# Attention and feed-forward on one core: additions at a batch's end in later steps, and products that nobody reads at the kernel's end

## The chip, the cores and the metric

The kernel runs on one core of a Trainium2 chip. The metric is the device time of one execution in microseconds (us); lower is better. Engine names follow the profile: PE is TensorE's matrix products, PEld its weight loads, DVE is VectorE, ACT is ScalarE, POOL is GpSimd, SP is SyncE, which issues most DMAs.

## The reference

`x` is 8 batches of 1024 rows of 128 numbers, all in float32. Each row is normalised, and attention with 8 query heads and one shared key and value head, and a linear feed-forward sum over 8 experts, are both added to the row:

```python
xn = _layernorm(x, axis=-1)
Q = jnp.einsum('bnd,hdk->bhnk', xn, proj_q)      # 8 heads
K = jnp.einsum('bmd,dk->bmk', xn, proj_k)
V = jnp.einsum('bmd,dv->bmv', xn, proj_v)
weights = softmax(jnp.einsum('bhnk,bmk->bhnm', Q, K), axis=-1)
O = jnp.einsum('bhnm,bmv->bhnv', weights, V)
attn = jnp.einsum('bhnv,hdv->bnd', O, proj_o)
mid = jnp.einsum('amh,ehn->aemn', xn, w1)        # no activation in between
ffn = jnp.einsum('aemn,enh->amh', mid, w2)
out = x + attn + ffn
```

Shapes: `proj_q`, `proj_o` (8, 128, 128), `proj_k`, `proj_v` (128, 128), `w1` (8, 128, 512), `w2` (8, 512, 128).

## The kernel before

Weights are multiplied together once at the start: queries and keys into one matrix per head (`wqk`), values and output into one per head (`wvo`), all experts into one 128x128 matrix (`wf`). After that the work is a single loop over 512 steps: 8 batches x 8 heads (a head of a batch is a unit `u`) x 8 blocks of 128 rows. The order of the instructions on every engine is the order in which the code writes them; nothing is rearranged by a scheduler, and semaphores are set by the framework.

Step `i` does, in this order:

- `logits(i)`: TensorE multiplies one block of 128 query rows with 1024 keys (`logits_half` twice, recorded at helper line L103) into a score tile `pl` in PSUM; VectorE takes the row maximum (`row_max`, L354); ScalarE computes the exponents and their sum (`exponents`, L360, with a second small instruction that reads the accumulated sum).
- `weights_t(i - 1)`: VectorE turns the divided rows of the step before in 32x32 blocks (L377). Every fourth step SP then moves the blocks with 16 DMAs (L405) into the tiles `g0` and `g1`.
- `divide(i)`: VectorE takes the reciprocal of the sums (L370), ScalarE multiplies the rows by it (L371).
- `run(...)`: TensorE takes the next one or two pairs of products from a list of jobs, 12 steps behind (`LAG`). The product of weights and values is cut into seven block products in place of eight, so POOL forms sums and differences of `g0` and `g1` (`sum_early` L423, `sums_late` L428, L429, L431), and the products (L453) of all heads of a batch gather in four PSUM accumulators, `acc0` to `acc3`. `PAIRS = (2, 2, 1, 2)` says how many pairs a step takes.
- every eighth step `queries` for the unit after next (copied out by ScalarE at L305), and four steps later `values` (copied out at L323 and L324).
- `collect(b, n)`: additions that bring the accumulators of a finished batch together.

Scores, queries and values share the PSUM pool `ps_sc`, which has two slots, used in turn (`slot`). `queries` and `values` stand behind the logits of their step, so the logits of the next step get the slot of the logits just before.

A column half is 64 of the 128 columns of the stationary matrix: `both_halves` writes the lower and the upper 64 output partitions with two products. `lo` and `hi` are these partitions in `collect` as well.

The end of batch `b` is counted by `b, r = divmod(i - 69, 64)`. Step `r` runs the parts that `COLLECT` lists, last in the step:

```python
COLLECT = {0: [0], 2: [1], 3: [2, 3], 4: [4], 6: [5], 7: [6, 7, 8], 8: [9], 10: [10], 11: [11]}
```

Parts 0 and 2 are copies on ScalarE; all others are additions on VectorE of one PSUM and one SBUF operand, 64 partitions by 512. Part 5 adds the lower half of `acc1` (L531), 6 its upper half (L533), 7 its lower half into upper partitions (L535); 8 and 9 (L538, L540) read the lower half of `acc2`, 10 (L542) its upper and 11 (L544) its lower half again. Part 7 reads what 6 wrote, 8 what 5 wrote, 9 what 7 wrote, 10 what 6 wrote, 11 what 10 wrote. At r = 15 the sums are turned and moved, and later added to `x` and stored. The table applies to batches 0 to 6. For batch 0, r = 6 is step 75; `values` stands in step 76 (r = 7), `queries` in step 80 (r = 11).

The last batch ends in `last_rows`: eight transposes (L622) and four products with `spread` (L631) into four PSUM tiles, additions to `x` (L638), and two DMAs out for each half, issued by SP and ACT (L643). They are the last work of the kernel; then the closing of the framework (L881) waits for all engines and landings.

Of the kernel before, what the change touches and what calls it, by code (L numbers as in the profile page):

```python
# [9 lines left out]
F32 = mybir.dt.float32  # L10
# [7 lines left out]
def kernel(  # L18
# [42 lines left out]
    nc = tc.nc  # L61
    ctx.enter_context(tc.manual_schedule())
    P = 128
    HP = P // 2
# [5 lines left out]
    NE, _, NF = w1.shape  # L70
    NB = S // P
    GN = 4
    GS = GN * P
# [16 lines left out]
    ps_acc = ctx.enter_context(tc.tile_pool(name="ps_acc", bufs=1, space=PSUM))  # L90
# [22 lines left out]
    xs, xns, xnTs, qTs, vfs = {}, {}, {}, {}, {}  # L113

    def chunked(t):

        return t.rearrange("(c p) d -> p c d", p=P)

    def rows_tile(name):
        return rows.tile([P, NB, D], F32, tag="rows", name=name)  # L120
# [50 lines left out]
    for e in range(2):  # L171
# [6 lines left out]
    ident = const.tile([P, P], F32, tag="ident", name="ident")  # L178
# [6 lines left out]
            name=nc.get_next_instruction_name(), act_func_set_id=EXP_AND_LN, ins=[], outs=[]  # L185
# [239 lines left out]
    def sums_late(u, engine):  # L425
        x1, x2 = key_half(g0s[u], 0), key_half(g0s[u], 1)
        y1, y2 = key_half(g1s[u], 0), key_half(g1s[u], 1)
        engine.tensor_sub(x1, y1, x1)  # L428
        engine.tensor_sub(x2, f1s[u], y1)  # L429
        f4s[u] = form("f4", u)  # L430
        engine.tensor_sub(f4s[u], y2, x2)  # L431
# [62 lines left out]
    def in_order(t):  # L494
        return t.rearrange("p (r t q) -> p t r q", r=NQ, q=Q)

    def by_query(t):
        return t.rearrange("p (t r q) -> p t r q", t=GN, q=Q)

    def collect(b, n):  # L500

        if n == 0:
            tiles = [rows_tile(f"end{k}_{b}").rearrange("p a b -> p (a b)") for k in range(2)]
            ends[b] = [t[:, ts(k, GS)] for t in tiles for k in range(2)]
            ends[b].append(late.tile([P, GS], F32, tag="end", name=f"end_{b}"))
            ys[b] = tiles[1]
        p1, c1, y0, y1, c2 = (by_query(t) for t in ends[b])
        p4, p21, p75, p63 = ((b, k) for k in (3, 0, 1, 2))

        def top(k):  # L510
            return in_order(accs[k][lo])

        def bot(k):
            return in_order(accs[k][hi])

        add = nc.vector.tensor_add
        if n == 0:
            nc.scalar.copy(c1[lo], bot(p4))
        elif n == 1:
            add(c1[lo], top(p4), c1[lo])  # L520
            del accs[p4]
        elif n == 2:
            nc.scalar.copy(p1[hi], bot(p21))
            nc.scalar.copy(p1[lo], bot(p21))
        elif n == 3:
            add(c1[lo], bot(p21), c1[lo])
        elif n == 4:
            add(y1[lo], top(p21), p1[lo])
            del accs[p21]
        elif n == 5:  # L530
            add(c1[lo], top(p75), c1[lo])  # L531
        elif n == 6:
            add(c1[hi], bot(p75), p1[hi])  # L533
        elif n == 7:
            add(c2[hi], top(p75), c1[hi])  # L535
            del accs[p75]
        elif n == 8:
            add(y0[lo], top(p63), c1[lo])  # L538
        elif n == 9:
            add(y0[hi], top(p63), c2[hi])  # L540
        elif n == 10:
            add(y1[hi], bot(p63), c1[hi])  # L542
        elif n == 11:
            add(y1[hi], top(p63), y1[hi])  # L544
            del accs[p63]
# [32 lines left out]
    def last_rows(b, run):  # L578

        add = nc.vector.tensor_add
        tiles = [rows_tile(f"end{k}_{b}").rearrange("p a b -> p (a b)") for k in range(2)]
        p1, c1, y, x_ = (by_query(t[:, ts(k, GS)]) for t in tiles for k in range(2))
        p63 = rows_tile(f"end2_{b}").rearrange("p a b -> p (a b)")[:, :GS]

        def top(k):  # L590
            return in_order(accs[b, k][lo])

        def bot(k):
            return in_order(accs[b, k][hi])

        nc.scalar.copy(c1[lo], bot(3))
        add(c1[lo], top(3), c1[lo])
        sums_late(B * H - 1, nc.vector)
        run(len(jobs) - 8)
        nc.scalar.copy(p1[lo], bot(0))  # L600
        nc.scalar.copy(p1[hi], bot(0))
        add(x_[lo], top(0), p1[lo])
        add(c1[lo], p1[lo], c1[lo])
        run(4)
        add(y[lo], top(1), c1[lo])
        add(x_[hi], bot(1), p1[hi])
        add(y[hi], top(1), x_[hi])
        run(4)
        for k, copy in enumerate((nc.vector.tensor_copy, nc.scalar.copy)):
            t = slice(2 * k, 2 * k + 2)  # L610
            copy(by_query(p63)[:, t], in_order(accs[b, 2])[:, t])
        pos = [ps_sc.tile([P, S // GN], F32, tag="sc", name=f"po_{b}_{c}") for c in range(2)]
        for c, k in ((2, 3), (3, 0)):
            del accs[b, k]
            pos.append(ps_acc.tile([P, S // GN], F32, tag=f"acc{k}", name=f"po_{b}_{c}"))
        pos = [t.rearrange("p (k g d) -> p k g d", k=2, g=2) for t in pos]
        x_b = xs.pop(b).rearrange("p (g t) (k d) -> p t k g d", g=2, k=2)
        for half in (range(0, 2), range(2, 4)):
            for c in half:
                for g in range(2):  # L620
                    first = (1 - g) * GS + c * P
                    nc.tensor.matmul(  # L622
                        pos[c][:, :, g],
                        lhsT=tiles[1][:, first : first + P],
                        rhs=ident,
                        is_transpose=True,
                        start=(g == 0),
                        stop=False,
                    )
            for c in half:  # L630
                nc.tensor.matmul(  # L631
                    pos[c].rearrange("p k g d -> p (k g d)")[:, HP:],
                    lhsT=p63[:, ts(c, P)],
                    rhs=spread,
                    start=False,
                    stop=True,
                )
                add(x_b[:, c], pos[c], x_b[:, c])  # L638
            for g, queue in enumerate((nc.sync, nc.scalar)):
                c = half[0]  # L640
                rows_ = chunked(out[b])[:, (1 - g) * GN + c : (1 - g) * GN + c + 2]
                src = x_b[:, c : c + 2, :, g].rearrange("p t k d -> p t (k d)")
                queue.dma_start(rows_, src)  # L643

    def one(t):
        return t.rearrange("p (c x) -> p c x", c=1)
# [86 lines left out]

    PAIRS = (2, 2, 1, 2)
    LAST_PAIRS = (2, 2, 1, 1, 1, 1, 1, 1, 1, 1, 1, 0)
    COLLECT = {0: [0], 2: [1], 3: [2, 3], 4: [4], 6: [5], 7: [6, 7, 8], 8: [9], 10: [10], 11: [11]}

    FIRST_ROWS = 4  # L740
    ROWS = {
# [25 lines left out]
    def run(n):  # L767
        for _ in range(n):
            job, *args = jobs.pop()
            job(*args)  # L770

    for i in range(NS):
# [15 lines left out]
        v, n = divmod(i - LAG, NB)  # L788
# [15 lines left out]
        if i % NB == GN and i >= LAG:  # L804
            s, r = divmod(i + 20, 32)
# [8 lines left out]
        for b in range(1, B):  # L814
            r = i - FIRST_ROWS if b == 1 else i - (b - 2) * H * NB - 44
            if r in ROWS:
                ROWS[r](b)
            r = i - 20 if b == 1 else i - (b - 1) * H * NB
# [4 lines left out]
        b, r = divmod(i - 23, H * NB)  # L823
# [4 lines left out]
        b, r = divmod(i - 69, H * NB)  # L828
        if 0 <= b:
            for n in COLLECT.get(r, ()):  # L830
                collect(b, n)
# [14 lines left out]
    sum_early(LAST, nc.vector)  # L846
    run(len(jobs) - 12)
    last_rows(B - 1, run)
    assert not jobs and not ends and not xs and not es

# [35 lines left out]
```

## Time and profile before

| What | Before |
|---|---|
| Time, median of 3 runs | 1913.11 us (1912.96 to 1914.8) |
| Span of the profiled execution, first to last instruction | 1911.0 us |
| Granted TensorE clock, mean | 1.000 |
| PE busy | 1905.4 us (100%), 8994 products |
| VectorE busy | 1410.2 us (74%) |
| ScalarE busy | 1356.1 us (71%) |
| POOL busy | 1402.1 us (73%) |
| Maximum of a block's rows (L354) | 1223 ns x 512 |
| Exponents of a block (L360) | 1113 ns x 512, and 192 ns for the sum |
| One `collect` addition | 663 to 695 ns, 7 of each |

The profiled execution's own time is its span, 1911.0 us; the times of the runs also hold what lies around the instructions, 2.1 us at the median. Starts are counted from the span's beginning. An f32 product shows as two records of PE, one for each pass. A line's "idle before" names what ended the engine's idle time in front of those instructions. In a timeline a row is: start, duration, engine, line, operation, output and inputs, shapes, count. An engine whose name ends in q is the engine's queue of commands, with its waits.

### The profile page before, as it was taken

The page shows a single profiled execution, that of the slowest core. Times are in us where ns is not written, and L with a number is a line of the kernel's source. Part 1 is how long each engine was busy: PE and PEld are TensorE (multiplying, and loading weights), DVE is VectorE, ACT ScalarE, POOL GpSimd, SP SyncE. Part 2 cuts the span into 40 slices and gives each one's busy share as a digit, 9 for nine tenths or more (in the row PEclk, how much of TensorE's full clock was granted, in tenths as well). Part 3 has the DMA queues.
Part 4 walks back from the last instruction along what each step waited for, and adds up shares of the span by engine and source line. Part 5 has one row for each costly group of instructions (what it writes and reads, how often), then busy time and mean ns, then how long its engine had stood idle before and what let it go on. Part 6 is the DMA issues. An engine that isn't in the chain of part 4 may idle for free.

```text
span 1911.0 us, 26803 instructions
## 1 busy us (share of the span) xinstructions
PE 1905.4 (100%) x8994; PEld 646.3 (34%) x8994; DVE 1410.2 (74%) x1779; ACT 1356.1 (71%) x1823; POOL 1402.1 (73%) x592
## 2 busy tenths in 40 slices
PE   9999999999999999999999999999999999999999
PEld 4333333333333333333333333333333333333333
DVE  8767778677786777777777776777678766787777
ACT  7677677776776777777676777777777776777674
POOL 2877877688676886777967768777687777677763
PEclk9999999999999999999999999999999999999999
DMA  6666676676767766677667776776767667666675
GB/s 200 155 154 148 143 155 153 144 171 150 158 141 156 171 150 147 151 159 167 145 147 158 158 166 138 157 158 144 179 139 156 149 148 173 137 144 146 155 174 133
DMA packets 140713, 295.07 MB, mean 154 GB/s; under 512 B 41120, under 2 KB 74656, under 8 KB 140064
## 3 DMA queue, kind: packets, MB, share of 16 engines
q1 hardware_dynamic: 139744, 292.96, 68.2%
q8 instruction: 72, 1.18, 0.3%
q14 instruction: 65, 0.53, 0.1%
q10 hardware_dynamic: 832, 0.39, 0.1%
HBM read 13.76 MB, written 4.19 MB: 9 GB/s over the span
## 4 chain that ended last, share of the span: by engine, by line
PE 78%; POOL 9%; SPq 5%; DVE 3%; ACT 2%; DMA 2%; issue 1%; POOLq 0%; DVEq 0%
PE pl L103 37%; PE acc L453 32%; SPq L405 5%; PE pq L103 4%; PE pv L103 4%; POOL f L431 2%; POOL g L428 2%; POOL g L429 2%; DMA g<-turned 2%; DVE nmax L354 1%; ACT e L360 1%; DVE turned L377 1%; PE acc L486 1%; ACT e L371 1%; DVE scratch_vf L224 0%
## 5 line engine op out<-in xcount | busy, mean ns | idle before, releaser
L103 PE MATMUL pl<-xnT,qT 128*64 128x512 f32 x4096 | 966.5, 592 | 0.5 <-DVE xnT L294 0.2
L354 DVE TENSOR_REDUCE nmax<-pl 128x1 f32<-128x1024 f32 x512 | 626.3, 1223 | 403.6 <-PE pl L103 402.6
L360 ACT ACTIVATE e<-pl,nmax 128x1024 f32<-128x1024 f32 x512 | 570.1, 1113 | 399.9 <-DVE nmax L354 399.9
L453 PE MATMUL acc<-g,vf 128*64 128x512 f32 x2536 | 843.3, 592 | 0.0
L371 ACT ACTIVATE e<-e,rinv 128x1024 f32<-128x1024 f32 x512 | 588.1, 1149 | 116.5 <-DVE rinv L370 116.4
L377 DVE STREAM_TRANSPOSE turned<-e 128x1024 f32<-128x1024 f32 x512 | 633.8, 1238 | 13.7 <-ACT e L371 2.2
L103 PEld LDWEIGHTS pl<-xnT,qT 128*64 128x64 f32 x4096 | 292.8, 137 | 585.5 <-issue 534.3
L453 PE MATMUL acc<-f,vf 128*64 128x512 f32 x1016 | 487.2, 592 | 0.0
L428 POOL TENSOR_TENSOR g<-g,g 128x2048 f32<-128x2048 f32 x63 | 287.1, 4558 | 260.8 <-DMA g<-turned 127.1
L453 PEld LDWEIGHTS acc<-g,vf 128*64 128x64 f32 x2536 | 247.6, 137 | 506.5 <-issue 503.9
L423 POOL TENSOR_TENSOR f<-g 128x2048 f32<-128x2048 f32 x63 | 287.2, 4558 | 174.3 <-PE acc L453 86.2
L431 POOL TENSOR_TENSOR f<-g,g 128x2048 f32<-128x2048 f32 x63 | 287.8, 4569 | 4.9
L429 POOL TENSOR_TENSOR g<-f,g 128x2048 f32<-128x2048 f32 x63 | 286.9, 4554 | 0.0
L453 PEld LDWEIGHTS acc<-f,vf 128*64 128x64 f32 x1016 | 139.2, 137 | 0.0
L103 PE MATMUL pq<-xnT,wqk 128*64 128x512 f32 (+1 forms) x516 | 121.5, 589 | 0.1
L103 PE MATMUL pv<-wvo,xnT 128*64 128x512 f32 x512 | 120.8, 592 | 0.0
L370 DVE RECIPROCAL rinv<-sums 128x1 f32<-128x1 f32 x512 | 83.8, 164 | 42.9
L360 ACT ACTIVATION_READ_ACCUMULATOR e<-pl,nmax 128x1 f32 x512 | 98.3, 192 | 0.0
L327 POOL TENSOR_TENSOR vf<-vf 128x256 f32<-128x256 f32 x64 | 46.9, 733 | 31.1 <-ACT vf L324 31.1
L305 ACT COPY qT<-pq 128x1024 f32<-128x1024 f32 (+2 forms) x66 | 63.6, 963 | 0.0
L103 PEld LDWEIGHTS pv<-wvo,xnT 128*64 128x64 f32 x512 | 37.2, 137 | 72.7 <-issue 69.4
L103 PEld LDWEIGHTS pq<-xnT,wqk 128*64 128x64 f32 x516 | 36.9, 137 | 71.9 <-issue 71.3
(100 smaller groups left out, 534.0 us busy)
## 6 DMA issues: line engine op xcount, KB each, us to landing
g<-turned SPq DMA_DIRECT2D x2028, 128.0 KB, 2.4
xn<-in_L_attn_x_dram SPq DMA_DIRECT2D x7, 512.0 KB, 4.6
xnT<-xnt SPq DMA_DIRECT2D x112, 32.0 KB, 1.9
out<-yt SPq DMA_DIRECT2D x112, 32.0 KB, 1.9
x<-in_L_attn_x_dram SPq DMA_DIRECT2D x6, 512.0 KB, 4.2
out_dram<-x SPq DMA_DIRECT2D x6, 512.0 KB, 5.1
scratch_g<-in_L_ffn_w_dram SPq DMA_DIRECT2D x2, 1024.0 KB, 8.4
scratch_f<-in_L_ffn_w_dram SPq DMA_DIRECT2D x2, 1024.0 KB, 12.6
```

The lines of the kernel that those rows point to most:

```text
L103: nc.tensor.matmul(dst[r], lhsT=lhsT[:, r], rhs=rhs, start=start, stop=stop)
L354: nc.vector.reduce_max(nmaxs[i], pls[i], AX.X, negate=True)
L360: nc.scalar.activation(es[i], pl, AF.Exp, bias=nmax, accum_out=sums[i])
L370: nc.vector.reciprocal(rinv, sums.pop(i))
L371: nc.scalar.mul(es[i], es[i], rinv)
L377: nc.vector.transpose(turned[k].rearrange("p k c t q -> p c k t q")[:, :, :, j, :], es.pop(i).rearrange("p (c k q) -> p c k q", k=NQ, q=Q),)
L405: nc.sync.dma_start(*ends_of(r, d))
L423: engine.tensor_add(f1s[u], key_half(g0s[u], 0), key_half(g0s[u], 1))
L428: engine.tensor_sub(x1, y1, x1)
L429: engine.tensor_sub(x2, f1s[u], y1)
L431: engine.tensor_sub(f4s[u], y2, x2)
L453: nc.tensor.matmul(accs[b, acc][ts(half, HP)], lhsT=vfs[u // GN][:, u % GN, f, c, :], rhs=w[:, :, c, :], start=(h == 0 and c == first), st ...
```

## The change

Two edits. The table of `collect` is written anew for r = 6 to 9. A new function, `spare_products`, is called as the last statement of `last_rows`, behind the last transposes and the last DMAs out; it takes the tags `acc1` and `acc2` for two PSUM tiles and multiplies parts of the identity with parts of the last batch's normalised, transposed rows, in tiles of 64x64 (`quarters`: two row halves by two column halves, each row half into its own tile) and 128x64 (`halves`). Nothing reads the results.

```diff
--- before.py
+++ after.py
@@ last_rows
                 queue.dma_start(rows_, src)
-
-
+        spare_products(b)
+
+    def spare_products(b):
+
+        pts = [ps_acc.tile([P, GS], F32, tag=f"acc{k}", name=f"pspare_{b}_{k}") for k in (1, 2)]
+        xn = xnTs[b]
+
+        def quarters(n):
+            for r in range(2):
+                for c in range(2):
+                    nc.tensor.matmul(
+                        pts[r][ts(c, HP), :n],
+                        lhsT=ident[ts(r, HP), ts(c, HP)],
+                        rhs=xn[ts(r, HP), :n],
+                        start=True,
+                        stop=True,
+                    )
+
+        def halves(n):
+            for c in range(2):
+                nc.tensor.matmul(
+                    pts[c][ts(c, HP), :n],
+                    lhsT=ident[:, ts(c, HP)],
+                    rhs=xn[:, :n],
+                    start=True,
+                    stop=True,
+                )
+
+        quarters(GS)
+        quarters(GS)
+        halves(P)
+        quarters(P)
@@
-    COLLECT = {0: [0], 2: [1], 3: [2, 3], 4: [4], 6: [5], 7: [6, 7, 8], 8: [9], 10: [10], 11: [11]}
+    COLLECT = {0: [0], 2: [1], 3: [2, 3], 4: [4], 7: [5, 6], 8: [7, 8], 9: [9], 10: [10], 11: [11]}
```

Here `P` is 128, `HP` 64 and `GS` 512.

## The prediction

> **What bounds the kernel now.** I read the page's busy shares first, then the timeline of each engine around one batch end (batch 0, steps 75 to 82, 289 to 312 us), then the closing records.
>
> ```profile
> PE 1905.4 (100%) x8994; PEld 646.3 (34%) x8994; DVE 1410.2 (74%) x1779; ACT 1356.1 (71%) x1823; POOL 1402.1 (73%) x592
> L103 PE MATMUL pl<-xnT,qT 128*64 128x512 f32 x4096 | 966.5, 592 | 0.5 <-DVE xnT L294 0.2
> ```
>
> TensorE is busy all through. Two things hide in that line. 512 score steps of four products leave 4096 records, so an f32 product is two passes. A record lasts 592 ns, but a pair of passes (lower and upper 64 columns) follows the last pair after 0.43 us. A wait below 0.16 us can't be seen as idle time; spacings show it. So I read starts:
>
> ```profile
> 292.24 1.89 PE L103 MATMUL pv<-wvo,xnT 128*64 128x512 f32 x8
> 294.17 1.94 PE L103 MATMUL pl<-xnT,qT 128*64 128x512 f32 x8
> ...
> 307.09 1.89 PE L103 MATMUL pq<-xnT,wqk 128*64 128x512 f32 x8
> 308.81 1.89 PE L103 MATMUL pl<-xnT,qT 128*64 128x512 f32 x8
> ```
>
> Eight passes start 1.72 us apart (307.09 to 308.81). Logits of step 77 should have started at 293.95 and did at 294.17: 0.22 us lost, and 0.05 more on its second pair (1.94 for 1.89). That is at r = 7 to 8 of the batch end. The score slots explain it: there are two, used in turn. Behind `values` (step 76) and behind `queries` (step 80) the next logits take the slot of the logits just before, so they wait until those are exponentiated. These are the two tight places of a batch end. With 0.04 us at step 75, the seven batch ends lose about 7 x 0.31 = 2.2 us, and between the first 60 us and the last ten nothing else is lost. More than 2.2 us (0.11%) cannot be won from this edit.
>
> VectorE, in order, says why step 77 was late:
>
> ```profile
> 291.00 0.16 DVE L370 RECIPROCAL rinv<-sums 128x1 f32<-128x1 f32 x1
> 291.08 0.66 DVE L531 TENSOR_TENSOR end<-acc,end 64x512 f32<-64x512 f32 x1
> 291.67 1.20 DVE L354 TENSOR_REDUCE nmax<-pl 128x1 f32<-128x1024 f32 x1
> ...
> 294.15 0.16 DVE L370 RECIPROCAL rinv<-sums 128x1 f32<-128x1 f32 x1
> 294.34 0.69 DVE L533 TENSOR_TENSOR end<-acc,end 64x512 f32<-64x512 f32 x1
> 295.07 0.68 DVE L535 TENSOR_TENSOR end<-acc,end 64x512 f32<-64x512 f32 x1
> 295.78 0.68 DVE L538 TENSOR_TENSOR end<-acc,end 64x512 f32<-64x512 f32 x1
> 296.39 1.21 DVE L354 TENSOR_REDUCE nmax<-pl 128x1 f32<-128x1024 f32 x1
> ```
>
> Addition 5 (L531) stood between the reciprocal of step 75 and the maximum of step 76, whose logits were long there. Now the stretch before the second tight place:
>
> ```profile
> 299.78 1.23 DVE L354 TENSOR_REDUCE nmax<-pl 128x1 f32<-128x1024 f32 x1
> ...
> 302.28 0.16 DVE L370 RECIPROCAL rinv<-sums 128x1 f32<-128x1 f32 x1
> 302.36 1.20 DVE L354 TENSOR_REDUCE nmax<-pl 128x1 f32<-128x1024 f32 x1
> ...
> 305.03 0.69 DVE L542 TENSOR_TENSOR end<-acc,end 64x512 f32<-64x512 f32 x1
> 305.75 1.23 DVE L354 TENSOR_REDUCE nmax<-pl 128x1 f32<-128x1024 f32 x1
> ```
>
> Step 78 has no addition in it: its reciprocal and the next maximum overlap.
>
> **Durations for the chain.** Maximum to exponent start 1.24 to 1.26 us (305.75, 307.01); exponent start to the end of its accumulator read 1.20 (307.01 to 308.22); that to the waiting logits 0.06 (294.11, 294.17); maximum start to the end of the same step's reciprocal 2.65 (299.78 to 302.44). From there to the next maximum: -0.08 with nothing between; 0.51 with one addition to the lower 64 partitions (291.16 to 291.67); 0.75 with one to the upper 64, which neither overlaps what is before nor what is behind it (304.99 to 305.75); 2.08 with additions 6, 7, 8, so 1.35 with 7 and 8 alone (2.08 less 0.73).
>
> **The moved additions.** By the diff four move, not five: 5 from r = 6 to 7, 7 and 8 from 7 to 8, 9 from 8 to 9; 6 stays in 7, behind 5. Nothing is added to or taken from VectorE's work; only which maximum waits changes.
> - r = 6 is empty: the maximum of step 76 starts at 291.08, not 291.67; its accumulator read ends at 291.08 + 1.24 + 1.20 = 293.52, before TensorE asks at 293.95. Won: 0.27 us.
> - r = 7, additions 5 and 6: over by 295.1. Logits of step 77 are done at 295.89, so that maximum waits for TensorE as it should. Reciprocal over at 298.54.
> - r = 8, additions 7 and 8: maximum of step 78 at 298.54 + 1.35 = 299.89 (was 299.78). Its slot is asked for again at 303.4; it is free at 302.3. Reciprocal over at 302.54.
> - r = 9, addition 9, where nothing was: maximum of step 79 at 302.54 + 0.75 = 303.29 (was 302.36). Reciprocal over at 305.94.
> - r = 10, addition 10 unmoved: maximum of step 80 at 306.69 (was 305.75); accumulator read over at 306.69 + 1.25 + 1.20 = 309.14; logits of step 81 at 309.20. TensorE would be ready at 308.81 - 0.27 = 308.54. Lost: 0.66, and 0.05 on the second pair.
>
> Net 0.71 - 0.27 = +0.44 us a batch end, times 7 = **+3.1 us**. The spare time before was 308.81 - 308.28 = 0.53 us; addition 9 in step 78 spends 0.83 of it. Some seven links, each steady to 0.02 us, make 0.3 to 0.6 a batch end: 2.1 to 4.2 us.
>
> Behind it nothing piles up: the maximum of step 81 waits for TensorE in both kernels (1.61 us idle before 310.74). The transpose of step 79's rows goes 0.9 us late, and with it SP's 16 block copies (before: 308.40 to 318.79) and POOL's L428 (before: 320.93 to 325.48); the first product on the copied blocks runs at about 325, on L428's output at about 332. Covered by 4 us. The `queries` copy on ScalarE ends 0.9 late, at 311.4; its slot is asked for at 312.6. acc1's last reader ends at 299.3 and step 79 writes it at 302.8 at the earliest; acc2's last reader is addition 11, unmoved. All at nothing.
>
> **The spare products.** 14 products, 28 passes, last on TensorE. The last `spread` pass starts at 1906.94 (passes are 0.16 apart), so they start at 1907.10. None of them holds the additions and the last copies out, which wait on earlier passes. Cover is the landing of those copies:
>
> ```profile
> L881 SPq EVENT_SEMAPHORE  x7: 17/28/1518, 1908.2 to 1911.0; - x7
> ...
> L881 SPq DRAIN  x3: 7/7/7, 1910.3 to 1910.6; - x3
> ```
>
> SP's waits for landings run from 1908.2 to 1910.3; then the closing handshake takes 0.7 us. TensorE must be done by 1910.3. No record shows a 64x64 tile. Bounds from the nearest row, the two column halves side by side at 0.43 us for 512 columns:
> - Row halves overlap too: a set of four costs 0.86; 2 x 0.86 + 0.21 + 0.21 = 2.1 us, over at about 1909.7 with 0.3 for changes of tile shape (1904.13 to 1904.66 is 0.10 over the usual spacing) and 0.17 to drain. Cost nothing.
> - One pair at a time: 2 x 1.71 + 0.21 + 0.43 = 4.1 us, over at 1911.3 to 1911.6: +1.0 to +1.3.
> - One product at a time: 8 x 0.85 + 0.43 + 0.85 = 8.1 us: +5.2.
>
> I take the pairs, +1.1 us: that is what the row shows; four at once never occur.
>
> The Trainium skill speaks against this choice. "TensorEngine Tiling (Array Packing)", section Tiling Modes, says that 64x64 tiles are four and that different tiles load and multiply independently; it also says that a change of tiling mode drains the engine. By the first the spare products would cost nothing and the sum would be 3.1 us. No run here shows it yet.
>
> **Sum.** The profiled execution spans 1911.0 us; the median of the runs, 1913.11, lies 2.1 above it, which the change does not touch. 1911.0 + 3.1 + 1.1 = 1915.2 of span, 1917.3 as a run. 0.2%, about what a measurement of this kernel can tell from no change, is 3.8 us: the line is at 1916.9.
>
> **Rivals.**
> - A, as summed: 1917.3, from 1916.2 to 1918.6. Chance 0.46, about three quarters above the line.
> - B, all four tiles at once, the tail hidden, the stall behind `queries` as above: 1916.2, from 1915.2 to 1917.3. For it: the two passes of a product follow each other in program order, yet the other half's first pass runs beside the first, so TensorE looks past a blocked pass. Against it: no row. Chance 0.32, a quarter above the line.
> - C, not slower: the delay of r = 9 is absorbed. It decides at the accumulator read of step 80: if that ends by 308.5 instead of 309.14, the logits of step 81 do not wait and only the 0.27 is left: 7 x 0.27 = 1.9 us less, 1911.2, or 1912.3 with A's tail. For it: VectorE is idle 26% of the time. Against it: that idle time lies behind step 81, and every link is an observed spacing. Chance 0.10.
> - D, one 64x64 product at a time: 3.1 + 5.2, 1921.4. Chance 0.06.
> - Something unseen: 0.06, two thirds of it slower.
>
> Slower by over 0.2%: 0.36 + 0.08 + 0.06 + 0.04 = 0.54. Within: 0.10 + 0.24 + 0.09 = 0.43. Faster: 0.03. The range 1915.3 to 1918.8 holds A and B and leaves out C, D and half or more of the unseen, about 0.2.
>
> **What would show it.** Right: logits of step 77 start 1.72 us behind `values`; those of step 81 start about 2.4 us behind `queries` instead of 1.72, with a record of 1.94; a new row of TensorE waiting for ScalarE's L360 seven times; maxima of steps 79 and 80 about 0.9 us later against the step's logits. For the tail: four sets of starts 0.43 us apart per pair, TensorE's last record after 1911.3 (old clock), and SP's last wait ending on TensorE. Wrong: step 81 on time (C), or TensorE over before the copies land (B).

## The result and the profile after

The changed kernel took 1916.89 us at the median of 14 runs (1916.64 to 1918.61), the kernel before 1913.3 in the same sessions (1912.89 to 1914.8). The ratio is 1.0019, 95% interval [1.0011, 1.0026]: about 3.6 us slower, just under the line of 0.2% that the prediction drew, with the line inside the interval. The predicted time was 1917.3.

One thing about the runs has to be known to read the numbers below: the executions of each of these kernels gather in two groups some 1.5 us apart, so a median moves by up to that much with the share of the upper group, and I give the lowest run beside it (after: 1916.64 for 1912.89, +3.75). The profiled execution after spans 1916.0 us, 5.0 more than before; 1.25 us of that stand before step 75, where both kernels run the same instructions (last section).

The page after, busy shares and the score products, then the waits of TensorE (engine, line, waited for: total us, times, longest):

```profile
PE 1909.5 (100%) x9022; PEld 649.1 (34%) x9022; DVE 1411.3 (74%) x1779; ACT 1356.8 (71%) x1823; POOL 1402.0 (73%) x592
...
L103 PE MATMUL pl<-xnT,qT 128*64 128x512 f32 x4096 | 966.9, 593 | 3.8 <-ACT e L360 3.6
```

```profile
PE pl L103 <- ACT e L360: 3.6, 7, 0.5
```

VectorE's work is the same 1779 instructions. New is a wait of TensorE for ScalarE's exponents, seven times, once for each batch end. The 28 more records of TensorE are the spare products' passes.

TensorE's timeline in batch 0, which runs 1.25 us later here than before:

```profile
293.49 1.89 PE L103 MATMUL pv<-wvo,xnT 128*64 128x512 f32 x8
295.21 1.89 PE L103 MATMUL pl<-xnT,qT 128*64 128x512 f32 x8
...
308.08 1.89 PE L103 MATMUL pq<-xnT,wqk 128*64 128x512 f32 x8
310.48 1.94 PE L103 MATMUL pl<-xnT,qT 128*64 128x512 f32 x8 [0.52 <-ACT e L360]
```

Both tight places have changed. Logits of step 77 start 1.72 us behind `values`: on time. Those of step 81 start 2.40 us behind `queries`, 0.68 late, and their record of 1.94 shows the 0.05 on the second pair. What they wait for is ScalarE's last instruction on step 80's scores, which ends at 310.43:

```profile
309.23 1.11 ACT L360 ACTIVATE e<-pl,nmax 128x1024 f32<-128x1024 f32 x1 [0.83 <-DVE nmax L354]
310.24 0.19 ACT L360 ACTIVATION_READ_ACCUMULATOR e<-pl,nmax 128x1 f32 x1
```

VectorE's timeline gives the chain that leads there:

```profile
297.14 1.23 DVE L354 TENSOR_REDUCE nmax<-pl 128x1 f32<-128x1024 f32 x1 [0.85 <-PE pl L103]
...
299.83 0.68 DVE L535 TENSOR_TENSOR end<-acc,end 64x512 f32<-64x512 f32 x1
300.55 0.68 DVE L538 TENSOR_TENSOR end<-acc,end 64x512 f32<-64x512 f32 x1
301.16 1.21 DVE L354 TENSOR_REDUCE nmax<-pl 128x1 f32<-128x1024 f32 x1
...
303.83 0.69 DVE L540 TENSOR_TENSOR end<-acc,end 64x512 f32<-64x512 f32 x1
304.55 1.23 DVE L354 TENSOR_REDUCE nmax<-pl 128x1 f32<-128x1024 f32 x1
...
307.24 0.69 DVE L542 TENSOR_TENSOR end<-acc,end 64x512 f32<-64x512 f32 x1
307.97 1.23 DVE L354 TENSOR_REDUCE nmax<-pl 128x1 f32<-128x1024 f32 x1
...
312.47 1.23 DVE L354 TENSOR_REDUCE nmax<-pl 128x1 f32<-128x1024 f32 x1 [1.13 <-PE pl L103]
```

The maximum of step 77 (297.14) waited for TensorE. From there to that of step 80 (307.97) no gap between two instructions of VectorE is longer than 0.12 us; the next maximum waits for TensorE again. Counted from one batch end to the next (the same product of steps 75 and 139) the period is 235.96 us for 235.49 before, 0.47 a batch end, 3.3 us for seven.

The kernel's end:

```profile
1911.17 0.82 PE L631 MATMUL po<-spread,end 128*128 128x192 f32 x4
1911.92 1.95 PE L654 MATMUL pspare<-xnT,ident 64*64 64x512 f32 x16
1913.80 0.44 PE L664 MATMUL pspare<-xnT,ident 128*64 128x128 f32 x4
1914.17 0.45 PE L654 MATMUL pspare<-xnT,ident 64*64 64x128 f32 x8
```

The 16 passes at 512 columns end 1.95 us after their first start: four groups of four, 0.43 us apart (0.48 for the first). Four tiles run at once. From the last `spread` pass to the end of the span it is 4.32 us, before 4.07: 0.25 more.

### The profile page after: what moved, and what is told of

It is laid out like the page before. It is cut to its first block, busy times and chain, and to the rows that moved or that the text cites. A ratio compares the mean times of both kernels' runs of the same rounds, so it can differ in the third digit from the quotient of the medians.

```text
span 1916.0 us, 26874 instructions
## 1 busy us (share of the span) xinstructions
PE 1909.5 (100%) x9022; PEld 649.1 (34%) x9022; DVE 1411.3 (74%) x1779; ACT 1356.8 (71%) x1823; POOL 1402.0 (73%) x592
## 4 chain that ended last, share of the span: by engine, by line
PE 94%; DVE 4%; ACT 1%; DMA 1%; issue 0%; SPq 0%; ACTq 0%; DVEq 0%
PE pl L103 43%; PE acc L453 38%; PE pv L103 6%; PE pq L103 5%; DVE nmax L354 1%; ACT e L360 1%; DVE turned L377 1%; PE acc L486 1%; DMA g<-turned 1%; PE pwf L103 0%; DVE end L542 0%; DVE end L540 0%; DVE end L535 0%; DVE end L538 0%; SPq L405 0%
```

## The experiments

Each was timed against the kernel before in the same session; the two sessions gave 1913.07 (lowest 1912.72) and 1913.16 (1912.83) for it.

| Kernel | Median, us | Lowest, us | Ratio [95%] | Late at step 77 / 81 in the profile, us |
|---|---|---|---|---|
| changed kernel | 1916.89 | 1916.64 | 1.0019 [1.0011, 1.0026] | 0 / 0.68 |
| new table alone | 1917.56 | 1916.03 | 1.002 [1.0012, 1.0029] | 0 / 0.68 |
| addition 9 back in r = 8 | 1916.44 | 1915.97 | 1.0018 [1.0009, 1.0026] | 0 / 0.67 |
| 5 to 7 in r = 7, 8 and 9 in r = 8 | 1911.29 | 1911.01 | 0.9991 [0.9982, 1.0] | 0 / 0 |
| new table, addition 10 in r = 11 | 1911.18 | 1910.94 | 0.9989 [0.998, 0.9998] | 0 / 0 |
| addition 5 alone moved | 1911.23 | 1910.98 | 0.999 [0.9981, 0.9999] | 0 / 0 |
| spare products alone | 1913.64 | 1913.1 | 1.0002 [0.9993, 1.0011] | 0.22 / 0 |
| spare products on two tiles | 1914.64 | 1914.47 | 1.0006 [0.9997, 1.0016] | 0.22 / 0 |
| twice the spare sets at 512 columns | 1914.51 | 1914.41 | 1.0006 [0.9997, 1.0015] | 0.22 / 0 |

The differences are small beside the intervals: those of the last three kernels include 1, and the three faster ones stop at 1.0 or just short of it. For these six the traces decide, by the waits that are there or not there.

**The table alone.** The changed kernel without `spare_products`.

> The new table of collect alone, without the spare products. Theory 1 (the wait behind queries at step 81 is the whole change): each of the seven batch ends is 0.47 us longer, as in the changed kernel (235.96 us from one batch end to the next for 235.49), 3.3 us in all: 1916.4 to 1916.8. Theory 2 (the spare products at the end cost about 1 us of the 3.6 measured): about 1915.5 to 1915.8.

Lowest run 1916.03, 3.3 us over the kernel before. In its profile the logits of step 81 start at 309.25 behind `queries` at 306.85, 2.40 us, as in the changed kernel. The table makes nearly the whole difference.

**Addition 9 back in r = 8.**

```diff
-    ... 7: [5, 6], 8: [7, 8], 9: [9], 10: [10], 11: [11]}
+    ... 7: [5, 6], 8: [7, 8, 9], 10: [10], 11: [11]}
```

> The new table, but addition 9 back in step r = 8: 7: [5, 6], 8: [7, 8, 9], and r = 9 empty. Theory 1 (between the maximum of step 77, which waits for TensorE, and that of step 80 the chain of VectorE and ScalarE has no slack, so that only the number of additions in between counts, four here as in the change): maximum of step 80 still late, logits of step 81 still start about 2.4 us behind queries, +3.3 to +3.7 us, 1916.4 to 1917. Rival, as the prediction put it (addition 9 in step 78, where nothing stood, spends the spare time): step 81 is on time again and the 0.27 us of step 77 are won, -1.9 us, 1911.3.

It is as slow as the change. Its VectorE timeline from the maximum of step 77 to that of step 80:

```profile
296.33 1.23 DVE L354 TENSOR_REDUCE nmax<-pl 128x1 f32<-128x1024 f32 x1 [0.86 <-PE pl L103]
...
300.46 0.69 DVE L540 TENSOR_TENSOR end<-acc,end 64x512 f32<-64x512 f32 x1
301.18 1.23 DVE L354 TENSOR_REDUCE nmax<-pl 128x1 f32<-128x1024 f32 x1
...
303.67 0.16 DVE L370 RECIPROCAL rinv<-sums 128x1 f32<-128x1 f32 x1
303.75 1.20 DVE L354 TENSOR_REDUCE nmax<-pl 128x1 f32<-128x1024 f32 x1
...
306.42 0.69 DVE L542 TENSOR_TENSOR end<-acc,end 64x512 f32<-64x512 f32 x1
307.15 1.23 DVE L354 TENSOR_REDUCE nmax<-pl 128x1 f32<-128x1024 f32 x1
```

Step 78 holds no addition again (303.67, 303.75), but the maximum of step 78 starts 0.8 us later than in the change, and that of step 80 comes 10.82 us after that of step 77, where the change has 10.83. Where in the stretch addition 9 stands makes no difference; that there are four additions in it (7 to 10, as in the change) does. The rival, which is how the prediction named the cause, is refuted.

**Three additions in the stretch.** From r = 7 on the table reads:

```diff
+    ... 7: [5, 6, 7], 8: [8, 9], 10: [10], 11: [11]}
```

> A table with r = 6 empty as in the change, but only three additions behind the maximum of step 77: 7: [5, 6, 7], 8: [8, 9], 10 and 11 as they were. Theory 1: additions 5 to 7 end at about 295.8 (old clock), before the logits of step 77 are done at 295.9, so they cost nothing; the three others make the accumulator read of step 80 end at about 308.3, before 308.5: neither logits 77 nor logits 81 wait. 7 x 0.27 = 1.9 us less than before: 1911.2 to 1911.5. Rival (any shift of the additions costs, as VectorE has no room in these steps): no better than before.

```profile
307.29 1.89 PE L103 MATMUL pq<-xnT,wqk 128*64 128x512 f32 x8
309.01 1.89 PE L103 MATMUL pl<-xnT,qT 128*64 128x512 f32 x8
```

1911.29: neither step waits; the logits of step 81 start 1.72 us behind `queries`. The stretch holds three additions, 8, 9 and 10. Additions 5 to 7 end at 296.21 and the maximum of step 77 starts at 296.35, 1.93 us after its logits did (294.42), which is TensorE's own pace. The rival is refuted.

**Addition 10 behind the stretch.** The changed table with one more move.

```diff
+    ... 7: [5, 6], 8: [7, 8], 9: [9], 11: [10, 11]}
```

> The changed kernel's table with one more move: addition 10 from r = 10 to r = 11, so that the maximum of step 80 has nothing ahead of it. Theory 1: its accumulator read ends at 308.3 instead of 309.1, step 81 does not wait, additions 10 and 11 end at 310.0 before the logits of step 81 are done; -1.9 us, 1911.2 to 1911.5. Rival (the lateness was made in step 78 by addition 9 and stays): still some +2 to +3 us.

```profile
305.91 0.16 DVE L370 RECIPROCAL rinv<-sums 128x1 f32<-128x1 f32 x1
305.99 1.21 DVE L354 TENSOR_REDUCE nmax<-pl 128x1 f32<-128x1024 f32 x1
...
309.39 0.68 DVE L544 TENSOR_TENSOR end<-acc,end 64x512 f32<-64x512 f32 x1
310.59 1.23 DVE L354 TENSOR_REDUCE nmax<-pl 128x1 f32<-128x1024 f32 x1 [0.52 <-PE pl L103]
```

With nothing before the maximum of step 80, the change turns from 3.3 us lost to 1.8 won (lowest run 1910.94). Additions 10 and 11 fit into VectorE's wait for the logits of step 81, of which 0.52 us are left. The additions 7, 8 and 9 stand where the change puts them, three in the stretch, so none of them alone makes the loss.

**Addition 5 alone moved**, to r = 7. The rest of the table is as before:

```diff
+    ... 7: [5, 6, 7, 8], 8: [9], 10: [10], 11: [11]}
```

> The old table with addition 5 alone moved, from r = 6 to r = 7: 7: [5, 6, 7, 8], 8: [9]. Theory 1: the logits of step 77 start on time (0.27 us won a batch end); the maximum of step 77 starts 0.5 us after its logits are done, but the chain up to step 80 holds two additions behind it (9 and 10) and its accumulator read ends at about 308.2, before 308.5. -1.9 us, 1911.2 to 1911.5. Rival (the move of 5 by itself costs): as before or slower.

1911.23, lowest 1.85 us under the kernel before. This is the part of the change that wins, by itself: a batch end takes 235.23 us for 235.49, and 7 x 0.26 = 1.8. The stretch holds two additions, 9 and 10, behind a maximum of step 77 that comes 0.5 us late.

**The spare products alone**, with the old table.

> The spare products alone, with the old table. Theory 1 (four tiles of 64x64 run side by side and end before the last copies out have landed): no change, within 0.1 us of before by the closing, 1913.0 to 1913.4. Theory 2 (pairs, as the prediction summed): 1914.2 to 1914.6.

1913.64; the lowest run is 0.27 over that of before, and the span ends 4.31 us after the last `spread` pass instead of 4.07. TensorE is done 3.03 us after that pass. SP's wait for the last landings ends at 3.27 (before: 3.15), and what it waits for is a copy, not TensorE:

```profile
SPq L911 <- DMA out_dram<-x: 1.8, 1, 1.8
```

So the closing is 0.25 us longer though it does not wait for TensorE's work. About half of the 0.25 is the landing, 0.12 later. The other half is SP's steps from there to the end of its waits: four short ones, one of them for TensorE, where the kernel before has two. SP's issue of the last copies is slower too, first in the kernel before, then in the changed kernel (1.62 us here):

```profile
1906.67 1.47 SPq L643 DMA_DIRECT2D out_dram<-x  x2
```

```profile
1911.40 1.61 SPq L643 DMA_DIRECT2D out_dram<-x  x2
```

Why, and whether the landing is later for it, was not tried.

**The spare products on two tiles**, with the old table.

```diff
-                        lhsT=ident[ts(r, HP), ts(c, HP)],
-                        rhs=xn[ts(r, HP), :n],
+                        lhsT=ident[ts(0, HP), ts(c, HP)],
+                        rhs=xn[ts(0, HP), :n],
```

> The old table and the spare products, but both row halves of quarters read rows 0 to 63, so that all its products fall on two tiles of 64x64 instead of four. This is the price of pairs that the prediction took. Theory 1: starts come in pairs, 0.43 us apart; quarters takes 1.71 us instead of 0.86 at 512 columns; TensorE ends 1.9 us later than with four tiles and the closing waits for it, about +1.4 to +1.7 us against the old kernel's closing in the trace. Rival (row halves do not matter, or TensorE's end is not waited for): no change against the spare products on four tiles.

```profile
1909.03 3.65 PE L654 MATMUL pspare<-xnT,ident 64*64 64x512 f32 x16
1912.61 0.44 PE L664 MATMUL pspare<-xnT,ident 128*64 128x128 f32 x4
1912.98 0.65 PE L654 MATMUL pspare<-xnT,ident 64*64 64x128 f32 x8
```

The same 16 passes take 3.65 us in place of 1.95: pairs, as the prediction took them. TensorE is done 4.92 us after the last `spread` pass, SP waits for it, and the span ends 1.45 us later than with four tiles; lowest run +1.64 against before.

```profile
SPq L911 <- PE pspare L654: 1.3, 1, 1.3
```

So pairs would have been waited for, as predicted, though at some 1.6 us and not 1.1; the change does not run in pairs.

**Twice the sets on four tiles.** `quarters(GS)` four times, with the old table.

> The old table and the spare products with four sets of quarters at 512 columns instead of two, on four tiles. Theory 1: each set costs 0.86 us, TensorE ends 1.71 us later, and what lies beyond the cover shows: the cover left is 0.2 to 0.4 us, so +1.3 to +1.5 us at the closing. Rival (cover is wider than read, or nothing waits for TensorE): no change.

```profile
1907.34 3.66 PE L654 MATMUL pspare<-xnT,ident 64*64 64x512 f32 x32
```

32 passes in 3.66 us, 1.71 more than 16. The span ends 1.28 us later than with two sets: SP waits for TensorE until 4.74 us after the last `spread` pass. Of 1.71 us added, about 0.4 were covered: that is all the cover that the change left, the 0.40 us between TensorE's end (3.03) and the start of SP's wait for it (3.43).

## Why the prediction was right or wrong

**The size and the sign** held: 1917.3 predicted, 1916.89 measured, inside the range. But the sum was put together from one term that was right and one that was wrong.

**The moved additions: right, link by link.** Net +0.44 us a batch end was summed, 0.47 is what the period shows; 3.1 against 3.3 us. Step 77's 0.27 was won. Counted from the logits of step 75, the maximum of step 79 came 0.93 us later and that of step 80 0.95, for 0.93 and 0.94 summed; against their own logits, which come 0.27 earlier, they are 1.2 later and not the 0.9 that the list of signs gives. The logits of step 81 waited 0.68 for 0.66 summed. That each place's spacings could be added up rests on VectorE's fixed order, and on reading whether an addition writes the lower or the upper 64 partitions: 0.51 and 0.75 us between a reciprocal and the next maximum.

The Trainium skill has a reason for that difference, which I had not used: "VectorE: DVE Perf Modes", section Two Vector instructions with no wait between them, gives a model in which an instruction is held until all earlier ones on VectorE have finished when its input or its output starts in another group of 32 partitions than the last one that was read from, or written to, the same memory. The rows agree: the maximum starts 0.08 before the end of an addition to the lower half (L538, 300.55 + 0.68, then 301.16) and 0.03 behind one to the upper half (L540, 303.83 + 0.69, then 304.55).

**The reason given was too narrow.** The step "addition 9 in step 78 spends 0.83 of it", of the 0.53 us spare, has the right size but blames one addition. With 9 back in step 77 the loss stays. The prediction's own spacings say so too: put together for that table, with 2.08 us for three additions behind one reciprocal, they give an estimate of 0.56 us lost, for 0.67 measured. What the runs showed in its place: from the maximum of step 77, which waits for TensorE, to the exponents of step 80, each link of the chain of VectorE and ScalarE starts on the one before, and the stretch has room for three additions but not for four. The kernel before had two in it behind a start that was 0.5 us late, the change four.

**The spare products: the step that failed** is "I take the pairs, +1.1 us: that is what the row shows; four at once never occur." They do: four passes start together and the tail costs 0.25 us, with TensorE off the path. By the prediction's own sign, TensorE over before the copies land (3.03 against 3.27 us), this half was wrong. Rival B was the case that came true, but for those 0.25 us: it gave 1916.2, and the two measured terms give 1911.0 + 2.1 + 3.3 + 0.25 = 1916.65. The rule of "TensorEngine Tiling (Array Packing)", section Tiling Modes, that different tiles work independently, spoke against the pairs, and the measurement agrees with it. Absence of a row was taken for evidence; the row that the rival rested on, the second half's first pass beside the first half's, was the better guide.

That the sum still came within 0.4 us of the median is luck: the tail was 0.85 too dear, the additions 0.2 too cheap, and the median of 1916.89 lies 0.24 over what the measured terms give. The chances of 0.54 slower and 0.43 within, on both sides of a line at 1916.9, fit a time that lies on that line, but 0.36 of the 0.54 came from a tail that did not occur. Of the 2.1 us that the sum adds for what lies around the instructions, the runs show 1.8 (a span of 1915.1 in the run of 1916.89); the other 0.3 is that the profiled execution of the kernel before was shorter than its median run.

**C** (the delay absorbed) is refuted by the waits of TensorE, and **D** (one product at a time) by the four starts together.

## What to carry to other kernels

When an engine is off the critical path by its average (VectorE at 74%), find the stretches, between two of its waits for the engine that bounds the kernel, in which it has no gap, and count the movable work in each; spreading work evenly over steps can move it into such a stretch. Here one addition moved (5 to r = 7) wins 1.8 us, and the whole new table wins as much when one more (10) leaves the stretch. Work added behind the last result is nearly free (0.25 us here) only as long as it ends before the closing asks for it: 0.4 us of cover was left, and 1.71 us more work cost 1.3.

## What the runs showed of the hardware

- Four 64x64 float32 tiles, two row halves and two column halves with each row half writing its own tile of PSUM, take 0.43 us a pass for 512 columns all together, the same as two of them. The program writes the four products one after the other and each is two passes, yet the first passes of the four start within 0.02 us, and the second passes behind them.
- Going from 64x64 to 128x64 tiles and back costs little: the first start behind each change was 0.11 and 0.10 us over the usual spacing (0.43 us at 512 columns, 0.11 at 128), and the next one 0.05 over it.
- The start of two executions can differ. In the profile of the kernel before, the trace's clock record gives TensorE the full clock from 5.5 us on, in that of the changed kernel from 9.5 us, with the same instructions up to there. Four passes of the first scores take 1.03 us before and 1.32 after, eight passes for queries ahead of them 1.40 and 2.05. Step 75 then runs 1.25 us later; 0.46 of that is there at 4.4 us already, behind a wait for a DMA of the weights. The kernel on two tiles starts late in the same way (full clock from 10.4 us, step 75 later by 1.8), the table alone does not (from 4.5 us, 0.01). "TensorE: Matmul & The Clock Gate" in the Trainium skill, Part 1, calls the window of that gate free-running: it does not begin with the kernel. That fits, but was not tested.
